# Cross-attention on one core: batch results transposed by VectorE and ScalarE instead of TensorE

## The chip, the cores and the metric

The kernel runs on one core of one Trainium2 chip. The metric is the device time of one execution in microseconds. The kernel before takes 938.81 us, the median of three runs (938.34 to 940.67).

The engines of the core are named as the profile names them: PE is TensorE's matrix products (PEld its weight loads), DVE is VectorE, ACT is ScalarE, POOL is GpSimd, SP is SyncE, which issues most transfers.

## What is computed

The reference works on 16 batches of 100 rows of 640 numbers (`x`) and 722 context rows of 384 numbers. The last 4 context rows of a batch are taken off as extra tokens (`ca`), and 718 remain (`enc`). There are 8 heads of 80 columns.

```python
query = hidden_states @ Wq
keyt = enc @ Wk
valt = enc @ Wv
hs = _mha(query, keyt, valt)
ca_q1 = jnp.einsum('btc,th->bch', ca, Wq_ca)
ca_q1 = ca_q1[:, indices, :]
ca_hs1 = _mha(ca_q1, residual, residual)
ca_q2 = ca_hs1 @ Wq
ca_k2 = ca @ Wk_ca
ca_v2 = ca @ Wv_ca
ca_hs2 = _mha(ca_q2, ca_k2, ca_v2)
out = hs + ca_hs2
out = out @ Wout + b_out
out = out + residual
```

Everything is float32. What this text is about is the step between the last two parts: `hs + ca_hs2` of a batch lies with its 100 rows on partitions, and the product with `Wout` needs it transposed, with the 640 columns on partitions, in 5 chunks of 128.

## The kernel before

**The loop.** After a first part that loads and combines the weights, one loop runs over the batches (line 1195). The order of the instructions inside it is written out by hand: each engine runs its own queue in the order of the program text. Iteration b works on the scores of batch b, forms the values of batch b and the keys of batch b + 1, and puts away the result of batch b - 1 (`last`). Its order on TensorE is:

1. the scores of batch b in three groups (`scores`, L623); ScalarE copies them to SBUF (L634, L640);
2. small products of the second attention (`softmax2`, `products`; L811, L749);
3. in iterations 2 to 15: the transposes of batch b - 1's result (`last.transpose`, L931). Five products with an identity, one for each chunk of 128 columns, write one PSUM bank, `hst_ps`; ScalarE copies it into `hsT` (L944), in one copy, or in two where a block of 128 output rows ends inside the batch. Iteration 1 does this later, near its end, for batch 0;
4. values and keys, 15 + 15 block products of 4 matrix products each (`Values`, L443, and `Keys`, L474);
5. the last chunk of the keys (L568); after every third iteration or so, the output product of two blocks of 128 rows (`project_pair`, L1010); in odd iterations the queries of the next two batches (L544);
6. probabilities times values (L1410). VectorE divides by the sums into `hs` (L1424) and adds `hs2`, the result of the second attention (L1431).

**Values and keys.** The products of `V_PLAN` are called V0 to V14 here, those of `K_PLAN` K0 to K14. Each names a PSUM bank or pair of banks (A to E), into which it adds, and a place in `vs` or `kT`. After each product the bank's present sum is read: by a ScalarE copy where the place is written for the first time (L416), by a VectorE addition otherwise (L414). The next product on the same bank has to wait for that read. The banks in order are

- V: A, B, D, A, B, E, A, B, C, A, C, B, A, B, A
- K: A, B, D, A, B, A, E, B, A, B, C, A, C, B, A

ScalarE reads V0, V1, V2, V8, V9, V14 and K0, K1, K2, K8, K9, K14; VectorE reads the rest. Banks A and B of V are a pair from the pool that also holds the first and the third group of scores.

**The maximum.** While these run, VectorE forms the maximum over all keys of each query (`Maximum`, `top`): a transpose in 32x32 blocks (L675), reductions (L677 to L687), then ScalarE spreads the result (`spread`, L697), and VectorE transposes it back into `over` (L705). `subtract` takes `over` from the scores (L1217), `exponential` follows on ScalarE (L1225). The calls `top.go(n)` in the loop set where these steps stand, and `both(n)` issues n products of V and then n of K:

```python
top.go(3)
both(3)
now.scores2()
top.go(1)
both(2)
top.go()
both(2)
both(1)
now.softmax3()
now.values2()
```

The first `top.go(3)` goes as far as the reductions, `top.go(1)` is `spread`, and `top.go()` is `over`. `softmax3` ends with `p2` (L862), which `values2` on GpSimd needs (L876, L883); it fills `hs2`, a buffer of which there is one.

**The rest of `last`.** `hsT` has three buffers of 128 rows each. When two blocks are complete (`PAIRS`), GpSimd forms sums of them (`sums`, L991) and TensorE multiplies them by `Wout` (`project_pair`).

Of the kernel before, what the change touches and what calls it, by code (L numbers as in the profile page):

```python
# [8 lines left out]
F32 = mybir.dt.float32  # L9
# [5 lines left out]
B, S, H = 16, 100, 640  # L15
# [3 lines left out]
P = 128  # L19
HC = H // P  # L20
# [12 lines left out]
OC = [(r, P) for r in range(0, B * S - P - 64, P)] + [(B * S - P - 64, 64), (B * S - P, P)]  # L33
# [7 lines left out]
HT = NH * T  # L41
# [12 lines left out]
for h in range(NH):  # L54
    lo = h * D
    while lo < (h + 1) * D:
        c = lo // P
        hi = min((h + 1) * D, (c + 1) * P)
        PIECES.append((h, c, lo - h * D, lo - c * P, hi - lo))
        lo = hi  # L60
# [75 lines left out]
def kernel(  # L136
# [18 lines left out]
    nc = tc.nc  # L155

    const = ctx.enter_context(tc.tile_pool(name="const", bufs=1))
    inp = ctx.enter_context(tc.tile_pool(name="inp", bufs=2))
    qpool = ctx.enter_context(tc.tile_pool(name="qpool", bufs=1))
    main = ctx.enter_context(tc.tile_pool(name="main", bufs=1))  # L160
# [22 lines left out]
    turn = [0]  # L183
# [10 lines left out]
    def scores_tile(name):  # L194
        return main.tile([P, 2, ROWS], F32, tag="st", name=name, bufs=NP)

    def hs_tile(name):
        return main.tile([P, H], F32, tag="hs", name=name)

    def hs2_tile(name):  # L200
        return main.tile([P, H], F32, tag="hs2", name=name)

    def hsT_tile(name):
        return main.tile([P, HC, P], F32, tag="hsT", name=name, bufs=3)

    def xn_tile(name):
        return main.tile([P, H], F32, tag="xn", name=name, bufs=2)
# [50 lines left out]
        tc.keep_in_program_order(dma)  # L258


    wv_sb = const.tile([P, NF, H // 2], F32, name="wv_sb")
    wk_sb = const.tile([P, NF, 2, P], F32, name="wk_sb")
    wk4 = const.tile([P, CC, P], F32, name="wk4")
# [79 lines left out]
    for c in range(HC):  # L343
        first = c * P - HEADS[c][0] * D
# [13 lines left out]

    room_v = xn_tile("wv_there")
    wv_there = {5: bias[:, : H // 2], 14: bias[:, H // 2 :], 7: room_v[:, : H // 2]}  # L360
    m_sb = [t[:, : B * HT] for t in (hs_tile("m_0"), xn_tile("m_1"), hs2_tile("m_2"))]
    m_sb += [
        hsT_tile(f"m_{c}").rearrange("p c s -> p (c s)")[:, : B * HT] for c in range(3, HC)
    ]
# [528 lines left out]
    hsTs = {}  # L893

    spare = []

    class Last:
# [20 lines left out]
        def parts(self, n):  # L918
# [2 lines left out]
                return [(0, slice(0, H))]  # L921
            return [(64 * k, slice(k * (H // 2), (k + 1) * (H // 2))) for k in range(2)]

        def transpose(self, chunks=[(0, HC)]):
            b, hs = self.b, self.hs
            if not self.t_ps:
                self.t_ps = psumk(f"hst_ps_{b}")
            t_v = self.t_ps[:, : HC * S].rearrange("p (c s) -> p c s", c=HC)
            for c0, c1 in chunks:
                for c in range(c0, c1):  # L930
                    nc.tensor.transpose(  # L931
                        t_v[:, c], hs[:S, c * P : (c + 1) * P], ident[:S, :S]
                    )
                for r, (lo, n) in enumerate(OC):
                    first, end = max(lo, b * S), min(lo + n, (b + 1) * S)
                    if first >= end:
                        continue
                    if r not in hsTs:
                        hsTs[r] = (
                            spare[0].rearrange("p (c s) -> p c s", c=HC)  # L940
                            if r == len(OC) - 1
                            else hsT_tile(f"hsT_{r}")
                        )
                    nc.scalar.copy(  # L944
                        hsTs[r][:, c0:c1, first - lo : end - lo],
                        t_v[:, c0:c1, first - b * S : end - b * S],
                    )

# [134 lines left out]
    for n in range(HC):  # L1083
        for c in range(CC):
            for lo in (0, 64):
# [5 lines left out]
                    stop=(c == CC - 1),  # L1091
                )
    k2T, at = [], 0
# [12 lines left out]
    for c in range(HC):  # L1106
        m_ps = psum(f"m_ps_{c}")
        for n, heads in enumerate(HEADS):
# [5 lines left out]
                stop=(n == HC - 1),  # L1114
# [46 lines left out]
    for c in range(CC):  # L1161
        for n in range(2):
# [5 lines left out]
                stop=(c == CC - 1),  # L1168
# [17 lines left out]
    last, enc_next, second_next = None, load_rest(1, load_enc(1)), Second(1, xT)  # L1186
# [8 lines left out]
    for b in range(B):  # L1195
        p = b // 2
        e_in, now = enc, second
        enc, second = enc_next, second_next
        mine = Last(b)
# [55 lines left out]
        if b == 0:  # L1255
            second.scores1()
            m_next = load_m(b + 2)
            kk.go(3)
            top.go(3)
            first_values(3, e_in, (act, act), get=bank)  # L1260
            top.go(1)
            kk.go(2)
            now.scores2()
            first_values(0, e_in, (act, act), (0,), bank)
            top.go()
            kk.go(3)
            first_values(0, e_in, (act, act), (1,), bank)
            now.softmax3()
            kk.go(2)
            subtract(0)  # L1270
            exponential(0)
            kk.go(2)
            subtract(1)
            kk.go(3)
            exponential(1)
            second_next, enc_next = loads()
            less = subtract(2)
            exponential(2)
            last_keys(b + 1, enc)
            enc_next = load_rest(b + 2, enc_next)  # L1280
            keys(m_next)
            now.values2(less)
            enc_sums(enc_next)
            second.softmax1(4)
        elif b + 1 < B:
            if b > 1:
                last.transpose()
            vv = Values(b, e_in)

            def both(n):  # L1290
                vv.go(n)
                kk.go(n)

            forms = [wout_sb[:, 2 * i : 2 * i + 2, k * (H // 2) : (k + 1) * (H // 2)]
                     for i in range(2) for k in range(2)]
            if b == 2:
                for o, left, right in (
                    (forms[1], forms[1], forms[0]),
                    (wout2[:, 0], forms[3], forms[1]),
                    (wout2[:, 1], forms[2], wout2[:, 0]),  # L1300
                ):
                    nc.gpsimd.tensor_tensor(o, left, right, ALU.subtract)
            elif last.b - 1 in PAIRS:
                nc.gpsimd.tensor_tensor(wout2[:, 0], wout2[:, 0], forms[0], ALU.add)
            second.scores1(seen)
            if b == 1:
                now.load()
            last.load()
            top.go(3)
            both(3)  # L1310
            now.scores2()
            top.go(1)
            both(2)
            top.go()
            both(2)
            both(1)
            now.softmax3()
            if b == 1:
                nc.gpsimd.tensor_tensor(last.hs[:S], last.hs[:S], last.hs2, ALU.add)
            now.values2()  # L1320
            if last.b in PAIRS:
                last.sums()
            vv.go(2)
            kk.go(1)
            subtract(0)
            exponential(0)
            vv.go(1)
            subtract(1)
            vv.go(1)
            kk.go(2)  # L1330
            exponential(1)
            vv.go(1)
            kk.go(2)
            both(1)
            both(1)
            if b == 1:
                for f in list(wv_there):
                    nc.scalar.copy(wv_sb[:, W_AT[f]], wv_there.pop(f))
            second.load()
            if b == 1:  # L1340
                nc.gpsimd.dma_start(out=bias, in_=bout[0].partition_broadcast(P))
            second_next, enc_next = loads()
            if b + 2 < B:
                m_next = load_m(b + 2)
            subtract(2)
            exponential(2)
            last_keys(b + 1, enc)
            if b + 2 < B:
                enc_next = load_rest(b + 2, enc_next)
            if b == 1:  # L1350
                last.transpose()
            if last.b in PAIRS:
                second.softmax1(3)
                last.project_pair()
                if last.b == max(PAIRS):
                    nc.sync.dma_start(
                        out=forms[1],
                        in_=wout[: 2 * P, H // 2 :].rearrange("(c p) n -> p c n", p=P),
                    )
            second.softmax1()  # L1360
        else:
            room = enc_tile("spare").rearrange("p f k -> p (f k)")
            spare.extend(room[:, i * H : (i + 1) * H] for i in range(2))
            last.transpose()
            vv = Values(b, e_in)
            last.load()
            mine.load()
            top.go(3)
            vv.go(3)
            last.project_few(len(OC) - 2)  # L1370
            now.scores2()
            top.go(1)
            vv.go(2)
            top.go()
            vv.go(3)
            now.softmax3()
            now.values2()
            vv.go(2)
            subtract(0)
            exponential(0)  # L1380
            vv.go(5)
            for i in (1, 2):
                subtract(i)
                exponential(i)
            last.project()
# [7 lines left out]
        if 0 < b < B - 1:  # L1393
            second.exponentials1()

        mine.hs = hs = hs_tile(f"hs_{b}")
        hs2 = now.hs2
        for g in range(2):
            a_ps = psum1(f"a_ps_{b}_{g}")
# [5 lines left out]
            for h, i in order:  # L1405
# [3 lines left out]
                for lo, hi in QC:  # L1409
# [5 lines left out]
                        stop=(i == len(KC) - 1),  # L1415
# [14 lines left out]
            if b:  # L1430
                nc.vector.tensor_tensor(hs[:S, cols], hs[:S, cols], hs2[:, cols], ALU.add)  # L1431
        mine.hs2 = hs2
        last = mine

    last.project(range(1))
# [53 lines left out]
```

## Time and profile before

| | |
|---|---|
| median of three runs | 938.81 us |
| profiled execution | 940.45 us |
| its span | 938.7 us |
| TensorE transposes L931, all 80 | 9.8 us busy, 251 ns each |
| copies of their result L944, 29 | 0.19 to 0.60 us each |
| block transposes of the maximum L675, L705 (128x800) | 1.01 us each |
| additions in `hs`, L1431 | 0.49 us each |
| VectorE waits for the first scores, L1241 | 49.1 us in 16 waits |
| GpSimd waits for `p2`, L876 | 41.2 us in 9 waits |

The span is the time from the first to the last instruction of the program. Busy times are sums over the engine's instructions; products of TensorE overlap, so that their busy time is more than the distance from one to the next. In a timeline, a row is a run of like instructions: start, time that they took together, engine, line, operation, output and inputs, shape, how many; in brackets stands the idle time of the engine just before, and what ended it.

### The profile page before, as it was taken

To read this page: it belongs to the slowest core of one execution; us is meant where nothing else is said; L and a number is where in the kernel's file an instruction comes from. 1 tells how busy PE (TensorE), PEld (TensorE's weight loads), DVE (VectorE), ACT (ScalarE), POOL (GpSimd) and SP (SyncE) were. 2 spreads that over 40 slices of the span, in tenths; PEclk is the share of its full clock that TensorE was granted. 3 is DMA by queue.
4 is the path that set the end of the run, shared out by engine and by line. 5 is a ranking of instruction groups with operands and counts; after the bars stand their busy time and mean duration, and the time that the engine had idled before them with its cause. 6 is when DMAs were issued, how large, how long until landed. Compare 5 with 4: busy or idle time off the path is not lost.

```text
span 938.7 us, 25800 instructions
## 1 busy us (share of the span) xinstructions
PE 929.9 (99%) x11195; PEld 792.8 (84%) x11195; DVE 687.9 (73%) x1098; ACT 372.6 (40%) x615; POOL 671.8 (72%) x614
## 2 busy tenths in 40 slices
PE   8999999999999999999999999999999999999998
PEld 6997979797797979888798788988879888798866
DVE  3859794989739796685957859589783897738884
ACT  1235443434334343442424434254441534415341
POOL 5757998688937878496874968658795587956723
PEclk9999999999999999999999999999999999999999
DMA  8822022040300303031030401205030050310201
GB/s 258 264 84 75 25 78 63 8 146 2 106 26 21 106 12 120 2 106 49 29 102 3 124 31 30 75 1 153 3 101 31 1 153 2 102 44 2 81 16 44
DMA packets 49672, 62.82 MB, mean 67 GB/s; under 512 B 14072, under 2 KB 38200, under 8 KB 49560
## 3 DMA queue, kind: packets, MB, share of 16 engines
q1 hardware_dynamic: 45512, 51.49, 18.2%
q0 software_dynamic: 3024, 8.53, 2.9%
q8 instruction: 88, 1.44, 0.6%
q10 hardware_dynamic: 1024, 1.15, 0.4%
q14 instruction: 24, 0.20, 0.1%
HBM read 55.59 MB, written 5.57 MB: 65 GB/s over the span
## 4 chain that ended last, share of the span: by engine, by line
PE 96%; DVE 2%; issue 1%; DMA 1%; ACT 0%; POOL 0%; ACTq 0%; DVEq 0%
PE s_ps L623 12%; PE a_ps L1410 12%; PE v_psA L443 10%; PE v_psB L443 8%; PE kT_ps L568 8%; PE k_psA L474 7%; PE q_ps L544 7%; PE k_psB L474 6%; PE o_ps L1010 5%; PE v_psC L443 3%; PE k_psC L474 3%; PE y_ps L749 2%; PE v_ps L384 2%; PE v_psD L443 2%; PE v_psE L443 2%; PE k_psE L474 1%
## 5 line engine op out<-in xcount | busy, mean ns | idle before, releaser
L784 POOL TENSOR_TENSOR e<-ca,g 100x800 f32<-100x800 f32 x64 | 99.5, 1565 | 137.2 <-DVE most L1229 123.6
L876 POOL TENSOR_TENSOR hs<-vb,p 100x640 f32<-100x640 f32 x64 | 120.5, 1892 | 50.4 <-DVE p L862 41.2
L509 POOL TENSOR_TENSOR enc<-enc 128x240 f32<-128x240 f32 x135 | 104.5, 783 | 20.0 <-DMA enc<-in_enct 12.9
L1410 PEld LDWEIGHTS a_ps<-vs,st 120*36 120x36 f32 (+3 forms) x3072 | 109.2, 125 | 4.9 <-issue 4.8
L1410 PE MATMUL a_ps<-vs,st 120*36 120x81 f32 (+3 forms) x3072 | 111.9, 233 | 0.0
L443 PE MATMUL v_psA<-wv_sb,enc 128*120 128x320 f32 x352 | 109.5, 434 | 0.0
L1217 DVE TENSOR_TENSOR st<-st,over 120x1600 f32<-120x1600 f32 x48 | 104.4, 2177 | 0.0
L883 POOL TENSOR_TENSOR hs<-hs,hs 100x640 f32<-100x640 f32 x48 | 99.1, 2064 | 3.8
L623 PE MATMUL s_ps<-qp,kT 32*120 32x100 f32 x3072 | 98.9, 263 | 0.6 <-issue 0.6
L623 PEld LDWEIGHTS s_ps<-qp,kT 32*120 32x120 f32 x3072 | 96.0, 179 | 2.4 <-issue 1.0
L791 POOL TENSOR_TENSOR e<-e,e 100x800 f32<-100x800 f32 x48 | 92.3, 1923 | 3.8
L443 PE MATMUL v_psB<-wv_sb,enc 128*120 128x320 f32 x296 | 91.9, 433 | 0.0
L640 ACT COPY st<-s_ps 120x800 f32<-120x800 f32 x64 | 49.7, 829 | 100.4 <-PE s_ps L623 100.4
L474 PE MATMUL k_psA<-enc,wk_sb 128*128 128x240 f32 x360 | 87.7, 366 | 0.0
L1229 DVE TENSOR_TENSOR most<-most,st 120x800 f32<-120x800 f32 x64 | 67.7, 1058 | 23.3 <-ACT st L634 22.2
L1225 ACT ACTIVATE st<-st 120x1600 f32<-120x1600 f32 x48 | 73.8, 1538 | 22.9 <-DVE st L1217 22.9
L474 PEld LDWEIGHTS k_psA<-enc,wk_sb 128*128 128x128 f32 x360 | 68.2, 190 | 16.8 <-DVE kT L414 0.3
L443 PEld LDWEIGHTS v_psA<-wv_sb,enc 128*120 128x120 f32 x352 | 63.2, 183 | 22.6 <-issue 0.5
L474 PE MATMUL k_psB<-enc,wk_sb 128*128 128x240 f32 x300 | 73.1, 366 | 0.3 <-DVE sm L859 0.3
L443 PEld LDWEIGHTS v_psB<-wv_sb,enc 128*120 128x120 f32 x296 | 54.1, 183 | 21.9 <-DVE vs L414 0.4
L544 PE MATMUL q_ps<-xT,wq_sb 128*128 128x200 f32 x400 | 69.1, 333 | 0.0
L544 PEld LDWEIGHTS q_ps<-xT,wq_sb 128*128 128x128 f32 x400 | 67.8, 190 | 1.0 <-issue 0.5
(162 smaller groups left out, 1734.6 us busy)
## 6 DMA issues: line engine op xcount, KB each, us to landing
vb<-va_d POOLq DMA_DIRECT2D x32, 250.0 KB, 3.6
vb<-va_d SPq DMA_DIRECT2D x32, 250.0 KB
enc<-in_enct SPq DMA_DIRECT2D x30, 240.0 KB
enc<-in_enct SPq DMA_DIRECT2D x15, 360.0 KB
xT<-in_xt SPq DMA_DIRECT2D x8, 500.0 KB
rest<-in_enct SPq DMA_DIRECT2D x31, 120.0 KB
xn<-in_x SPq DMA_DIRECT2D x11, 320.0 KB
out<-xn SPq DMA_DIRECT2D x11, 320.0 KB
```

The costliest lines, as they stand in the source:

```text
L443: nc.tensor.matmul(at[0][j][:KN, : H // 2], a_form(self.enc, f)[:, j * KN : (j + 1) * KN], wv_there.get(f, wv_sb[:, W_AT[f]]), start=first ...
L474: nc.tensor.matmul(at[:, i * KT : (i + 1) * KT], wk_sb[:, W_AT[f], i], a_form(self.enc, f), start=(first and i == 0), stop=last, skip_grou ...
L509: nc.gpsimd.tensor_tensor(out, left, right, op)
L544: nc.tensor.matmul(q_ps[:, : 2 * S].rearrange("p (j s) -> p j s", j=2), wq_sb[:, c, n * P : (n + 1) * P], xT[:, :, c, :], start=(c == 0), ...
L568: nc.tensor.matmul(bank[:, i * KT : (i + 1) * KT], weights[c], a_raw(enc, u, c), start=(i == 0 and c == 0), stop=(c == CC - 1), skip_group ...
L623: nc.tensor.matmul(s_ps[r][:n, 256 * a + lo : 256 * a + hi], kT[rows, c, u, j * KN : (j + 1) * KN], rhs, start=(a == 0 and c == 0), stop=( ...
L784: first = nc.gpsimd.tensor_tensor(to, self.ca[:, t, :].unsqueeze(1).to_broadcast([S, NH, S]), g[:, :, t].unsqueeze(2).to_broadcast([S, NH, ...
L791: nc.gpsimd.tensor_tensor(e, e, to, ALU.add)
L876: first = nc.gpsimd.tensor_tensor(to, self.vb[t][:S].rearrange("p (h d) -> p h d", h=NH), p2[:, :, t].unsqueeze(2).to_broadcast([S, NH, D] ...
L883: nc.gpsimd.tensor_tensor(sums, sums, to, ALU.add)
L1217: return nc.vector.tensor_tensor(st[i], st[i], top.over[:KN].unsqueeze(1).to_broadcast([KN, 2, ROWS]), ALU.subtract,)
L1410: nc.tensor.matmul(a_v[lo:hi, h % 4], st[i // 2][: KEYS[i], i % 2, h * S + lo : h * S + hi], block(i, h // 4)[: KEYS[i], h % 4], start=(i ...
```

## The change

The results of batches 1 to 13 no longer go through TensorE.

- `hs` becomes one fixed tile, `hs_sb`, of 128 rows. Its rows from 96 on are cleared once in the columns that no early use of the tile fills (`m_0` of the first part lies in it).
- After the last addition to `hs` of batches 1 to 13, VectorE transposes the whole tile in 32x32 blocks into `turned`, which takes a buffer of the tag `hs2`.
- In iterations 2 to 14, ScalarE copies the blocks to their places in `hsT`: for each of the 4 groups of 32 rows and each of the 4 groups of 32 partitions, one copy of 32 partitions and 5 runs of up to 32 elements. A group of rows that lies across the end of a block of 128 output rows is copied in two parts.
- The call of `last.transpose()` at the beginning of iterations 2 to 14 goes. Batches 0, 14 and 15 are transposed as before.
- `place` stands behind `spread`. The two calls `both(2)` become one `both(4)`, and `top.go()`, which is `over`, comes behind it. This holds for iterations 1 to 14.

```diff
+    hs_sb = const.tile([P, H], F32, name="hs_sb")
+    nc.gpsimd.memset(hs_sb[96:, B * HT :], 0.0)
...
+        def turn(self):
+
+            self.turned = hs2_tile(f"turned_hs_{self.b}")
+            nc.vector.transpose(self.turned, self.hs)
+
+        def place(self):
+
+            turned = self.turned.rearrange("p (c m k) -> p c m k", m=4, k=32)
+            for i in range(4):
+                at = self.b * S + 32 * i
+                stop = min(at + 32, (self.b + 1) * S)
+                for r, (lo, n) in enumerate(OC):
+                    first, end = max(lo, at), min(lo + n, stop)
+                    if first >= end:
+                        continue
+                    for m in range(4):
+                        nc.scalar.copy(
+                            self.hsT(r)[32 * m : 32 * m + 32, :, first - lo : end - lo],
+                            turned[32 * i : 32 * i + 32, :, m, first - at : end - at],
+                        )
...
         elif b + 1 < B:
-            if b > 1:
-                last.transpose()
             vv = Values(b, e_in)
...
             both(3)
             now.scores2()
             top.go(1)
-            both(2)
+            if b > 1:
+                last.place()
+            both(4)
             top.go()
-            both(2)
             both(1)
             now.softmax3()
...
-        mine.hs = hs = hs_tile(f"hs_{b}")
+        mine.hs = hs = hs_sb
...
         mine.hs2 = hs2
+        if 0 < b < B - 2:
+            mine.turn()
         last = mine
```

`self.hsT(r)` gives the buffer of block r, as the lines that it replaces in `transpose` did.

## What the change does to the time: a prediction

> **What bounds the kernel now.** I read the engine totals first, then the chain that ended last, then the timelines of TensorE, VectorE and ScalarE in one iteration of the batch loop, iteration 4 (the one that works on batch 4 and puts away batch 3). The first view is parts 1 and 4 of the page.
>
> ```profile
> PE 929.9 (99%) x11195; PEld 792.8 (84%) x11195; DVE 687.9 (73%) x1098; ACT 372.6 (40%) x615; POOL 671.8 (72%) x614
> ...
> PE 96%; DVE 2%; issue 1%; DMA 1%; ACT 0%; POOL 0%; ACTq 0%; DVEq 0%
> ```
>
> TensorE (PE) is busy for 99% of the span, and 96% of the chain is TensorE. So a product taken off it shortens the run, unless another engine then makes it wait. The question is who stands next in line, and that is read from iteration 4. First TensorE's timeline (start, time, engine, line, operation):
>
> ```profile
> 281.33 0.59 PE L931 MATMUL hst_ps<-ident,hs 100*128 100x100 f32 x5
> 281.76 1.26 PE L443 MATMUL v_psA<-wv_sb,enc 128*120 128x320 f32 x4
> ...
> 287.44 1.24 PE L443 MATMUL v_psA<-wv_sb,enc 128*120 128x320 f32 x4
> 288.51 1.24 PE L443 MATMUL v_psB<-wv_sb,enc 128*120 128x320 f32 x4
> 289.59 0.97 PE L474 MATMUL k_psA<-enc,wk_sb 128*128 128x240 f32 x4
> 290.40 0.97 PE L474 MATMUL k_psB<-enc,wk_sb 128*128 128x240 f32 x4
> ...
> 292.29 1.24 PE L443 MATMUL v_psA<-wv_sb,enc 128*120 128x320 f32 x4
> 293.36 0.97 PE L474 MATMUL k_psA<-enc,wk_sb 128*128 128x240 f32 x4
> ```
>
> The five transposes show 0.59 us, but the next product starts 0.43 us after them: 281.33 to 281.76. That is what they hold TensorE. The rows from 287.44 are V3, V4, K3, K4, V6 and K5 of the two plans. A V product costs 1.08 us from start to start, a K product 0.81.
>
> VectorE's timeline of the same stretch:
>
> ```profile
> 288.99 0.81 DVE L414 TENSOR_TENSOR vs<-v_psA,vs 120x640 f32<-120x640 f32 x1
> 289.90 0.82 DVE L414 TENSOR_TENSOR vs<-v_psB,vs 120x640 f32<-120x640 f32 x1
> 290.67 0.66 DVE L414 TENSOR_TENSOR kT<-k_psA,kT 128x480 f32<-128x480 f32 x1
> 291.43 0.66 DVE L414 TENSOR_TENSOR kT<-k_psB,kT 128x480 f32<-128x480 f32 x1
> 292.01 1.00 DVE L705 STREAM_TRANSPOSE over<-spread 128x800 f32<-128x800 f32 x1
> 292.93 0.85 DVE L414 TENSOR_TENSOR vs<-v_psE,vs 120x320 f32<-120x320 f32 x2
> 293.89 0.83 DVE L414 TENSOR_TENSOR vs<-v_psA,vs 120x640 f32<-120x640 f32 x1
> ```
>
> V3 ended at 288.68 (287.44 + 1.24); VectorE reads it at 288.99, 0.31 us late, since it comes from the reduction of the maximum. It runs through without a pause. VectorE is thus a third of a microsecond behind TensorE, with no wait to be seen yet, because each bank has time until its next product.
>
> ScalarE's timeline, and two of its copies from SBUF to SBUF by source line (count: shortest/median/longest ns):
>
> ```profile
> 289.23 1.71 ACT L697 COPY spread<-mx 64x800 f32<-64x800 f32 x2
> 297.61 0.96 ACT L416 COPY vs<-v_psC 120x320 f32<-120x320 f32 x2 [6.67 <-PE v_psC L443]
> ```
>
> ```profile
> L697 ACT COPY spread<-mx x42: 841/856/862, 77.2 to 905.5; 64x800 f32<-64x800 f32 x42
> L1338 ACT COPY wv_sb<-bias x2: 460/460/461, 138.2 to 138.5; 128x320 f32<-128x320 f32 x2
> ```
>
> After `spread` ScalarE is idle for 6.67 us. The copies of `place` go into that gap.
>
> **What is removed.** Thirteen times five transposes (iterations 2 to 14). The trace gives 0.43 us from the first to the next product in each of these (0.49 in iteration 15, which keeps its own): 13 x 0.43 = 5.6 us at most. Not all of it can be had at once: V0 writes a bank pair whose last reader, ScalarE's copy of the scores at L640 (279.77 + 1.55 = 281.32), ends just where the transposes began. With 0.06 us from the end of a read to the next product (K12 in iteration 3 starts 0.05 after the read that it waited for), V0 can start 0.38 earlier, not 0.43. ScalarE loses its one or two copies at L944 (0.6 us); it is not on the path.
>
> The Trainium skill ("TensorE: Matmul & The Clock Gate", Part 4: PE-mode transpose) gives about 275 ns for a transpose inside a kernel. By that figure 65 of them would be an estimated 17.9 us; this trace has them 0.086 us apart, and the sum goes by the trace.
>
> **What is added.** (a) VectorE's `turn`, 128x640: the nearest row is the same operation on 128x800 (L675) at 1.01 us, so 0.81 us by size, 13 times. It stands behind the last addition to `hs`, where VectorE next waits 2.4 to 2.9 us for the first scores (L1241 in iterations 3 to 5). Cost nothing; without that cover 0.8 us on the maximum, hence on V3's read. (b) `place`: 16 copies of 32 partitions, 20 where a block of 128 rows ends inside the batch (it does in nine of thirteen; 244 in all). The two rows give (856 - 460)/480 = 0.83 ns an element and 0.196 us fixed. Four times 500 elements make 1.66 us; 20 fixed parts 3.9 us; in sum 5.6 us. The copies at L1338 start 0.36 apart though they last 0.46, so neighbours may overlap by 0.10: 3.7 us. The two at L697 do not overlap, so I take 5.6. It begins at 290.94 and ends at 296.5. Queued behind it on ScalarE are the two copies of V8's banks, which V10 waits for, then V9, K8 and the first exponential. V8 will come some 0.3 earlier, at 297.3: hidden. V10 starts at 299.5 or later and the two copies take 0.96, so `place` may last 7.5 us before TensorE waits: 0.38 us a copy. (c) GpSimd's `values2` writes the buffer that `turned` sits in, so it waits for `place`; but it waits for `p2` anyway, which ends after 298. Nothing. (d) A memset of 32x128 on GpSimd at the start: 32x800 takes 0.76 there (L368), so under 0.2 us; GpSimd then idles 9.8 us before L721. Nothing. No DMA is added or moved.
>
> **What is moved.** Two things, both in `both(4)`. VectorE's `over` goes behind K6's read, past V5, V6, K5 and K6; it is needed by the first `subtract`, which stays behind V7 and K7, so the order alone costs that nothing. And V5 and V6 go ahead of K3 and K4, on TensorE and on VectorE. That is the part that costs: K3's bank is wanted again by K5 after K4 alone, where before V5 and V6 lay between. In offsets from V0 in the before, K5 stands at 11.61 in both orders. VectorE's reads now run V3, V4, V5, V6, K3 and take 0.91 + 0.74 + 0.96 + 0.74 + 0.65 = 4.00 us from V3's start (spacings of rows as above; 0.74 from V4 to another target is iteration 3's, where nothing holds VectorE up). They start at 6.92 plus the lag. So K5 can start at 6.92 + lag + 4.00 + 0.06, and the gain that is left is 0.63 - lag, no more than 0.38. VectorE's start is set by the scores and does not come forward when the transposes go.
>
> The lags of V3's read, from the timelines: 0.30 to 0.32 in iterations 2, 4, 6 to 10, 12 and 14; 0.24 in 11, 0.26 in 13; 0.84 in 3, 0.73 in 5, where VectorE's maxima last 1.4 us instead of 1.0; 1.43 in 1. So: nine iterations at 0.32 make 2.9 us; iterations 11 and 13 give 0.38 and 0.37; iteration 3 loses 0.21 but no longer pays the 0.16 that its K12 waited; iteration 5 loses 0.10. Iteration 1 has no transposes to lose but takes the new order: K5 is 0.80 later, of which 0.35 was already paid at K6; 0.4 lost. Sum: 2.9 + 0.75 - 0.05 - 0.10 - 0.4 = 3.1 us.
>
> The profiled execution took 940.45 us (span 938.7 and 1.75 around it); it would take 937.3. The median of the three runs is 938.81, 0.17% lower; less 3.1 it is **935.7**.
>
> **A rule against the change.** The Trainium skill ("VectorE: DVE Perf Modes", rules for kernel authors) sends a 128x128 transpose to TensorE where its result may lie in PSUM, as it may here. Followed to the letter it would say to leave things alone: by the rows above, 0.43 us of TensorE and 0.6 of ScalarE become 0.8 of VectorE and up to 5.6 of ScalarE. Which counts depends on who is idle, and that the page does not weigh.
>
> **The rivals.**
> - *All of it comes through.* K5's wait does not show, because VectorE passes from bank to bank faster in the new order, and V0 starts at once. 13 x 0.43 = 5.6 us: 933.2. For it: at the typical lag the wait is under 0.1 us. Against it: ScalarE's copy ends only just before V0, and iterations 1, 3 and 5 are late.
> - *VectorE eats it.* If lags of 0.6, as between the typical and iterations 3 and 5, become the rule (GpSimd's sums fall elsewhere against VectorE's maxima), 0.63 - lag is nothing and iteration 1 still loses 0.4: 939.2. Against it: nine of thirteen lags agree within 0.02.
> - *ScalarE becomes the bound (slower).* Place: V10, waiting for V8's two copies behind `place`. Point: 0.38 us a copy; to be slower by 0.3% needs about 0.41. At 0.45, nine iterations wait 20 x 0.45 - 7.5 = 1.5 us, 13.5 in all, less 3.1: 949.2. For it: 0.196 us fixed, no overlap at L697, and no row of copies between unlike partitions. Against: the smallest copies of the trace (L944) take 0.19.
>
> **Chances.** Under 0.3%, 2.8 us, a measurement of this kernel can't be told from no change. My forecast has 0.50 with a range of its own of 934.4 to 936.9 (0.1 us more or less of lag in each of 13 iterations); 936.0 is the limit of faster, so 0.32 of it counts as faster and 0.18 as the same. All of it: 0.24. VectorE eats it: 0.09. ScalarE: 0.17. Faster 0.56, same 0.27, slower 0.17. The range goes from 932.9 (all of it, with 0.3 us of spread) to 939.8 (nothing left, with 1 us).
>
> **What would show it.** V0 follows the last y product with no row at L931 in iterations 2 to 14; a gap of up to 0.1 us before K5 at the typical lag, larger in iterations 1, 3 and 5; no idle time before V10; `place` ends before V8's copies; `turn` lies inside VectorE's wait for the first scores. A mean over 0.38 us from copy to copy, or a lag of V3's read that grows by more than the 0.38, proves me wrong.

## The result, and the profile after

| kernel | median | fastest to slowest | ratio |
|---|---|---|---|
| before | 939.61 us (7 runs) | 938.12 to 941.32 | |
| after | 942.87 us (7 runs) | 942.26 to 943.54 | 1.0035 [1.0023, 1.0046] |

The change makes the kernel slower by 0.35%, 3.3 us. I had forecast 935.7 us. The profiled execution of the kernel after took 943.54 us, with a span of 941.8 (before: 938.7). Some line numbers moved: V products are L442, K products L473, VectorE's reads of them L413, ScalarE's L415, `over` L704, `p2` L861, `subtract` L1240, `values2` L875 and L882, `turn` L935, `place` L948.

Parts 1 and 4 of the page of after:

```profile
PE 930.6 (99%) x11130; PEld 785.7 (83%) x11130; DVE 698.5 (74%) x1111; ACT 434.6 (46%) x836; POOL 674.1 (72%) x615
...
PE 85%; DVE 12%; issue 2%; ACT 1%; DMA 0%; POOL 0%; ACTq 0%; DVEq 0%
```

TensorE lost its 65 transposes, and ScalarE gained 62 us of copies. What tells most is the chain: VectorE's share went from 2% to 12%. TensorE now waits for it somewhere.

Where, the waits show (engine, tile and line; what it waited for; us in total, times, longest). In the before, no wait of a K product for VectorE sums to more than 0.3 us:

```profile
PE k_psA L473 <- DVE kT L413: 2.2, 6, 0.4
...
PE k_psC L473 <- DVE kT L413: 0.7, 2, 0.3
```

The list shows only part of it: it counts the time from the end of one row to the start of the next, and in an even pace these rows overlap by 0.16 us (a K product lasts 0.97 and the next starts after 0.81). Below, K4 ends at 459.88 and K5 starts at 459.99, 0.11 by that count, but 0.27 behind the pace. The timeline of TensorE in iteration 7 of after, in two stretches, K3 to K6 and V12 to K12 (the view ends inside K12, hence x3):

```profile
458.10 0.97 PE L473 MATMUL k_psA<-enc,wk_sb 128*128 128x240 f32 x4
458.91 0.97 PE L473 MATMUL k_psB<-enc,wk_sb 128*128 128x240 f32 x4
459.99 1.05 PE L473 MATMUL k_psA<-enc,wk_sb 128*128 128x240 f32 x4
460.87 0.97 PE L473 MATMUL k_psE<-enc,wk_sb 128*128 128x240 f32 x4
...
470.31 1.24 PE L442 MATMUL v_psA<-wv_sb,enc 128*120 128x320 f32 x4
471.38 0.97 PE L473 MATMUL k_psA<-enc,wk_sb 128*128 128x240 f32 x4
472.42 0.88 PE L473 MATMUL k_psC<-enc,wk_sb 128*128 128x240 f32 x3
```

A K product costs 0.81 us from start to start. K4 to K5 takes 1.08 and K5 to K6 0.88: 0.27 of waiting and 0.07 to regain the pace. K11 to K12 takes 1.04: 0.23 of waiting. VectorE in the same iteration, with everything between K3's read and K10's that matters here:

```profile
458.42 0.82 DVE L413 TENSOR_TENSOR vs<-v_psA,vs 120x640 f32<-120x640 f32 x1
459.18 0.66 DVE L413 TENSOR_TENSOR kT<-k_psA,kT 128x480 f32<-128x480 f32 x1
...
462.46 1.00 DVE L704 STREAM_TRANSPOSE over<-spread 128x800 f32<-128x800 f32 x1
...
465.10 0.19 DVE L861 TENSOR_TENSOR p<-e,sm 100x32 f32<-100x32 f32 x1
465.20 1.82 DVE L1240 TENSOR_TENSOR st<-st,over 120x1600 f32<-120x1600 f32 x1
468.22 2.85 DVE L1240 TENSOR_TENSOR st<-st,over 120x1600 f32<-120x1600 f32 x1
...
471.72 0.64 DVE L413 TENSOR_TENSOR kT<-k_psC,kT 128x480 f32<-128x480 f32 x1
```

K3's read ends at 459.84 and K5 starts at 459.99; K10's read ends at 472.36 and K12 starts at 472.42. Both waits are for the reads named. The first read is late because K3's product, which now stands behind V5 and V6, is done only at 459.07 (458.10 + 0.97); the read starts at 459.18, while V6's read (458.42) is still running. The second is late because it stands behind the second `subtract`, which ends at 471.07 (468.22 + 2.85).

The balance over all iterations, from the starts of the first scores product, of V0 and of K14 in both traces (after less before, us). Iteration 7 stands for 2, 4, 9, 10 and 12, all within 0.01:

| iteration | 1 | 3 | 5 | 6, 8 | 7 | 11 | 13 | 14 |
|---|---|---|---|---|---|---|---|---|
| scores to V0 | -0.03 | -0.43 | -0.14 | -0.43 | -0.43 | -2.24 | -0.80 | -0.43 |
| V0 to K14 | +1.11 | +0.67 | +1.25 | +0.34 | +0.64 | +0.68 | +0.76 | +0.95 |

The transposes bring 13 x 0.43 = 5.6 us, but the stretch from V0 to K14 loses 10.0 in the fourteen iterations. That makes +4.4. The rest is single pauses that differ between the two profiled executions: beyond their 0.43, iterations 11 and 13 show 2.2 us that the profile of before alone spent, in pauses of TensorE for which it names no cause ("issue"); after has one of 0.91 at the end of iteration 4 and loses 0.29 in iteration 5, and its loop starts 0.3 earlier. Together: +3.1, the difference of the spans.

### The profile page after: what moved, and what is told of

Read it like the earlier page. It is cut to its first block, busy times and chain, and to the rows that moved or that the text cites. A ratio compares the mean times of both kernels' runs of the same rounds, so it can differ in the third digit from the quotient of the medians.

```text
span 941.8 us, 25879 instructions
## 1 busy us (share of the span) xinstructions
PE 930.6 (99%) x11130; PEld 785.7 (83%) x11130; DVE 698.5 (74%) x1111; ACT 434.6 (46%) x836; POOL 674.1 (72%) x615
## 4 chain that ended last, share of the span: by engine, by line
PE 85%; DVE 12%; issue 2%; ACT 1%; DMA 0%; POOL 0%; ACTq 0%; DVEq 0%
PE a_ps L1432 12%; PE s_ps L622 11%; PE kT_ps L567 8%; PE v_psA L442 8%; PE q_ps L543 7%; PE v_psB L442 7%; PE k_psA L473 6%; PE o_ps L1033 5%; PE k_psB L473 5%; PE v_psC L442 3%; DVE vs L413 3%; DVE st L1240 2%; PE k_psC L473 2%; DVE most L1252 2%; PE v_ps L383 2%
## 5 line engine op out<-in xcount | busy, mean ns | idle before, releaser
L875 POOL TENSOR_TENSOR hs<-vb,p 100x640 f32<-100x640 f32 x64 | 119.8, 1881 | 53.1 <-DVE p L861 24.1
L442 PE MATMUL v_psA<-wv_sb,enc 128*120 128x320 f32 x352 | 110.0, 435 | 0.3
L1240 DVE TENSOR_TENSOR st<-st,over 120x1600 f32<-120x1600 f32 x48 | 107.1, 2234 | 0.0
L882 POOL TENSOR_TENSOR hs<-hs,hs 100x640 f32<-100x640 f32 x48 | 100.6, 2096 | 3.8
L442 PE MATMUL v_psB<-wv_sb,enc 128*120 128x320 f32 x296 | 91.8, 433 | 0.0
L473 PE MATMUL k_psA<-enc,wk_sb 128*128 128x240 f32 x360 | 88.7, 369 | 3.0 <-DVE kT L413 2.2
L473 PEld LDWEIGHTS k_psA<-enc,wk_sb 128*128 128x128 f32 x360 | 67.1, 190 | 22.3 <-issue 4.3
L442 PEld LDWEIGHTS v_psA<-wv_sb,enc 128*120 128x120 f32 x352 | 62.8, 183 | 24.4 <-DVE vs L413 2.9
L473 PE MATMUL k_psB<-enc,wk_sb 128*128 128x240 f32 x300 | 73.1, 366 | 0.3 <-DVE sm L858 0.3
L442 PEld LDWEIGHTS v_psB<-wv_sb,enc 128*120 128x120 f32 x296 | 54.1, 183 | 21.9 <-DVE vs L413 0.4
L1444 DVE RECIPROCAL rs<-a_ps 100x4 f32<-100x4 f32 x32 | 5.8, 180 | 86.0 <-PE a_ps L1432 86.0
```

Of the source, the lines that this page charges most:

```text
L442: nc.tensor.matmul(at[0][j][:KN, : H // 2], a_form(self.enc, f)[:, j * KN : (j + 1) * KN], wv_there.get(f, wv_sb[:, W_AT[f]]), start=first ...
L473: nc.tensor.matmul(at[:, i * KT : (i + 1) * KT], wk_sb[:, W_AT[f], i], a_form(self.enc, f), start=(first and i == 0), stop=last, skip_grou ...
L875: first = nc.gpsimd.tensor_tensor(to, self.vb[t][:S].rearrange("p (h d) -> p h d", h=NH), p2[:, :, t].unsqueeze(2).to_broadcast([S, NH, D] ...
L882: nc.gpsimd.tensor_tensor(sums, sums, to, ALU.add)
L1240: return nc.vector.tensor_tensor(st[i], st[i], top.over[:KN].unsqueeze(1).to_broadcast([KN, 2, ROWS]), ALU.subtract,)
```

## The experiments

Medians are set against the kernel before as measured beside them: 939.63 us (17 runs) for kernels 1 to 4 and 939.21 us (10 runs) for 5 to 8. "Kernel 1" is that of experiment 1, and so on. "Typical" is an iteration like 7.

**1. The change with the old order.** `place` and `turn` stay; the order of the products and of `over` is that of the before.

```diff
-            both(4)
-            top.go()
+            both(2)
+            top.go()
+            both(2)
```

> The changed kernel with the order of before: both(2), over, both(2), both(1); turn and place stay. Theory A (the new order costs): K5 and K12 wait no longer, so V0 to K14 lasts as before (27.5 us in most iterations) while the transposes stay away; 0.43 us in some ten of thirteen iterations, 934 to 935.5 us, ratio 0.994 to 0.996 of before. Rival B (the new work of VectorE and ScalarE costs, whatever the order): 942 to 943 us, as the changed kernel.

936.4 us, ratio 0.9964 [0.9951, 0.9978]: 3.2 us faster than before, 0.9 above the range that I expected. From V0 to K14 a typical iteration takes the time of the before to within 0.01, so it gains the whole 0.43; K5 stands 11.61 us after V0 and K12 23.74, as in the before. Not the full 5.6 us come, because iterations 3 (+0.64), 5 (+0.51), 11 (+0.55), 13 (+0.37), 14 (+0.35), 6 and 8 (+0.17) lose some from V0 to K14. In iteration 3, K6 waits 0.41 for V5's read and K12 0.29: V0 has come forward by 0.43 and VectorE, held by the maxima, has not. These losses come to 2.8 us. So it is the order that makes the change slow, not its new work.

**2. The order alone.** The kernel before, with `both(4)` and then `top.go()`, and TensorE's transposes kept.

```diff
-            both(2)
-            top.go()
-            both(2)
+            both(4)
+            top.go()
```

> The kernel before with the new order alone: both(4), over, both(1); transposes on TensorE, no turn, no place. Theory A: slower than before without any new work. Iteration 1 loses 1.1 us as in the changed kernel; in the others the lag of 0.31 leaves K5 free, but over comes later, p2 is 0.4 us later, GpSimd's values2 with it, and K12 waits 0.2 to 0.3 us; in all 3 to 5 us, 942.5 to 944.5 us. Rival B: the order costs iteration 1 alone, 939.5 to 940.7 us.

948.15 us, ratio 1.0094 [1.0079, 1.0109]: 8.5 us slower than before. Less the 5.6 us of the transposes that is 2.9, near the 3.3 of the whole change. It costs about twice what I expected, and I had K5 free. The reason is in TensorE's and VectorE's timelines of iteration 7 (K3, K4 and K5; the reads of V6 and K3):

```profile
459.75 0.97 PE L474 MATMUL k_psA<-enc,wk_sb 128*128 128x240 f32 x4
460.56 0.97 PE L474 MATMUL k_psB<-enc,wk_sb 128*128 128x240 f32 x4
461.64 1.05 PE L474 MATMUL k_psA<-enc,wk_sb 128*128 128x240 f32 x4
```

```profile
459.95 0.82 DVE L414 TENSOR_TENSOR vs<-v_psA,vs 120x640 f32<-120x640 f32 x1 [0.42 <-PE v_psA L443]
460.83 0.66 DVE L414 TENSOR_TENSOR kT<-k_psA,kT 128x480 f32<-128x480 f32 x1
```

V0 starts at 449.77 here, so V3's read (457.00) is 7.23 after it, as in the before: the lag is the old 0.31. Yet K5 waits 0.27. VectorE idles 0.42 us until V6's product is done, reads it by 460.77, and starts K3's read at 460.83. So VectorE is not late at all. It is K3's product that comes late: it ends at 460.72, and the read follows 0.11 behind it. In the eight iterations of after in which K5 starts 11.87 or 11.88 after V0 it is the same, though the lag is 0.73 there: V6's read starts between 10.29 and 10.30 after V0, in kernel 2 at 10.19, but K3's read always at 11.07, 0.11 after K3's product. (Where an idle VectorE waits for a product, as for V6's here, the read starts 0.04 after its end. The other 0.07 may be owed to V6's read in front; the traces don't tell.) So at lags from 0.22 to 0.74 the wait doesn't depend on the lag. The order of the products sets it: from the end of K3 to K5's due start there are 0.65 us, and a read takes 0.66.

**3. Only `over` late.** The change with V5, V6, K3 and K4 in the old order, and `over` behind K6.

```diff
-            both(4)
+            both(2)
+            both(2)
             top.go()
```

> The changed kernel with both(2), both(2), over, both(1): V and K products alternate as before, over alone stays late. Theory A in two parts: K5 does not wait (that part came from V5 and V6 ahead of K3), K12 still waits some 0.3 us (that part comes from the late over, through p2 and values2); 936.5 to 939 us. If the order of the products were all of the cost: 934 to 935.5. If over's place were all of it, or if it is rival B: 942 to 943.

937.69 us, ratio 0.9977 [0.9968, 0.9986], as expected: 1.3 us above kernel 1, where `over` is early, and 5.2 below after, where V5 and V6 go first. K5 stands at 11.61 again with no wait. But a typical iteration still loses 0.30 of its 0.43, and all of that at K12 (0.22 of waiting and 0.08 until the pace is back). VectorE and GpSimd in iteration 7:

```profile
459.25 1.00 DVE L704 STREAM_TRANSPOSE over<-spread 128x800 f32<-128x800 f32 x1
460.17 0.78 DVE L413 TENSOR_TENSOR vs<-v_psB,vs 120x640 f32<-120x640 f32 x1
460.88 0.64 DVE L413 TENSOR_TENSOR kT<-k_psB,kT 128x480 f32<-128x480 f32 x1
...
461.88 0.19 DVE L861 TENSOR_TENSOR p<-e,sm 100x32 f32<-100x32 f32 x1
461.99 1.82 DVE L1240 TENSOR_TENSOR st<-st,over 120x1600 f32<-120x1600 f32 x1
...
465.01 2.85 DVE L1240 TENSOR_TENSOR st<-st,over 120x1600 f32<-120x1600 f32 x1
```

```profile
462.21 3.96 POOL L875 TENSOR_TENSOR hs<-vb,p 100x640 f32<-100x640 f32 x2 [2.10 <-ACT vs L415]
466.25 3.02 POOL L882 TENSOR_TENSOR hs<-hs,hs 100x640 f32<-100x640 f32 x1
```

The same steps in iteration 7 of the before, where V0 starts at 445.15 (`p2`, the two `subtract`, `values2`):

```profile
461.49 0.19 DVE L862 TENSOR_TENSOR p<-e,sm 100x32 f32<-100x32 f32 x1
461.59 1.82 DVE L1217 TENSOR_TENSOR st<-st,over 120x1600 f32<-120x1600 f32 x1
...
464.91 2.55 DVE L1217 TENSOR_TENSOR st<-st,over 120x1600 f32<-120x1600 f32 x1
```

```profile
461.75 4.02 POOL L876 TENSOR_TENSOR hs<-vb,p 100x640 f32<-100x640 f32 x2 [2.19 <-DVE p L862]
```

In kernel 3 `over` now stands in front of V7's and K7's reads, and behind these stand the steps of `softmax3` that end in `p2` and the first `subtract`. With V0 at 445.24, `p2` starts 16.64 after V0 instead of 16.34. From there a fixed train runs. `values2` on GpSimd and the first `subtract` start behind `p2`, 0.22 apart (the profile names ScalarE as what `values2` waited for, since it also waits for `place`; but in kernels 1 and 3 and in after alike it starts 0.13 after `p2` ends); the two products of `values2` end 2.36 us after that `subtract` (466.17 after 463.81); the second `subtract`, begun while they run, ends 1.69 after them (467.86); K10's read follows. In the before the same distances are 2.36 and 1.69, in after 2.37 and 1.68. So whatever `p2` loses, K10's read loses: 0.30 here, 0.65 in after (0.30 from `over`, 0.35 from K5). In the before K12 came 0.13 after the read it needed, so there was little slack to eat. Over the whole program a late `over` costs less than 0.30 an iteration on average, because V5's read now goes ahead of it: K6 no longer waits in iterations 1, 3 and 5, and these are shorter than in kernel 1.

**4. `values2` behind the second `subtract`.** The change as it is, but GpSimd starts later.

```diff
             now.softmax3()
-            now.values2()
...
+            now.values2(subtract(1))
+            if last.b in PAIRS:
+                last.sums()
```

> The changed kernel, with GpSimd's values2 of iterations 1 to 14 held back until the second subtract has ended. Theory A: K12 waits because subtract and values2 run at the same time and hold each other up; then the second subtract falls from 2.85 to about 1.8 us and K12's wait goes (0.3 us in ten iterations), K5's stays: 939.5 to 940.5 us, unless the later hs2 makes the end of an iteration wait. If the subtract is long for another reason: 2.85 us and K12's wait stay, 942.5 to 944 us.

946.01 us, ratio 1.0065 [1.0051, 1.0078]. VectorE and GpSimd in iteration 7:

```profile
467.34 1.82 DVE L1240 TENSOR_TENSOR st<-st,over 120x1600 f32<-120x1600 f32 x1
470.36 1.81 DVE L1240 TENSOR_TENSOR st<-st,over 120x1600 f32<-120x1600 f32 x1
```

```profile
472.30 2.50 POOL L875 TENSOR_TENSOR hs<-vb,p 100x640 f32<-100x640 f32 x2 [7.21 <-issue]
474.89 1.54 POOL L882 TENSOR_TENSOR hs<-hs,hs 100x640 f32<-100x640 f32 x1
```

Apart from each other, the `subtract` takes 1.81 us, the two products 2.50 instead of 3.97, the sum 1.54 instead of 3.01. K12's wait is gone: a typical V0 to K14 loses 0.32 instead of 0.64, and that is K5's part (its wait stays, 0.26). The mechanism holds, but the total went the other way: the sums for `project_pair` now stand behind `values2`, and the output product of iterations 3, 6, 8, 11 and 13 takes 0.77 to 2.07 us longer, with waits for these sums (L1014) and for what GpSimd makes after them (L1054). (The profiled execution also has a pause of 1.45 us put down to "issue" ahead of V0 of iteration 3; it took 947.38, 1.4 above the median.)

**5. `over` between V5 and V6.** The order of kernel 1, but with V5, on TensorE and on VectorE, ahead of `over`:

```diff
-            both(4)
-            top.go()
+            both(2)
+            vv.go(1)
+            top.go()
+            vv.go(1)
+            kk.go(2)
```

> The run with the old order (936.4 us), with over moved behind V5's read alone: both(2), V5, over, V6, K5, K6, both(1). Theory A: the typical iteration stays as it is (no wait there); in iterations 1, 3, 5, 11 and 13, where VectorE is over 1 us late, K6 no longer waits for V5's read (0.3 to 0.5 us each) and p2 keeps its time; 934 to 935.5 us. If over's place mattered only through p2: 936.4 as before.

935.4 us, ratio 0.9961 [0.9949, 0.9974]: as expected, and the lowest median of all. Its chain by engine:

```profile
PE 95%; DVE 2%; POOL 1%; issue 1%; DMA 0%; ACT 0%; DVEq 0%; POOLq 0%
```

TensorE has nearly its share of the before again. V5's read ahead of `over` frees pair E for K6, so the late iterations gain too (iteration 1 -0.42 from V0 to K14 against the before, 3 -0.26, 5 -0.02). Some of it comes back in 3, 11 and 13, where the output product starts on time but takes 0.7 to 0.9 us longer. In iteration 3 it falls 0.42 behind its pace at a product that needs GpSimd's sums (L1014) and 0.32 at one that needs `wout2`, which GpSimd makes after them (L1054); that is all of its 0.74. Its interval overlaps that of kernel 1, so that it is better than kernel 1 is not shown by the times.

**6. The same, with `values2` late and the sums ahead of it.** The edit of kernel 4 on top of kernel 5, with `last.sums()` left where it was.

> The same, and GpSimd's values2 held back behind the second subtract, with the sums of the output pair ahead of it, so that project_pair needn't wait for them. Theory A: the second subtract takes 1.8 us instead of 2.5, K12's wait goes in iterations 3, 5, 11 and 13 (0.3 each), and the wait of 0.8 to 2 us behind K14 that values2's delay alone brought in iterations 3, 6, 8, 11 and 13 goes as well; 932.5 to 934.5 us. If hs2 comes too late now for the end of an iteration: 936 to 940.

935.81 us, ratio 0.9962 [0.9949, 0.9976]. A miss: no better than kernel 5. My premise was wrong: in kernel 5 K12 no longer waits in iterations 3, 5, 11 and 13 either, so that a typical iteration gains no more than 0.03 beyond its 0.43. And while the output product no longer waits for the sums, GpSimd's later step for it (L1054) now comes after the delayed `values2`: in iteration 6 it ends 11.01 us after K14's start, the product that needs it starts at 11.06, and the output product takes 0.2 to 0.6 us longer in the iterations that have one.

**7. `place` cut short.** Kernel 1 with one or two ScalarE copies of all 128 partitions in place of the 16 or 20; the output rows of batches 1 to 13 are then not those of the reference, since the blocks are not put in their places.

```diff
-                    for m in range(4):
-                        nc.scalar.copy(
-                            self.hsT(r)[32 * m : 32 * m + 32, :, first - lo : end - lo],
-                            turned[32 * i : 32 * i + 32, :, m, first - at : end - at],
-                        )
+            nc.scalar.copy(
+                self.hsT(r)[:, :, first - lo : end - lo],
+                turned[:, :, first - self.b * S : end - self.b * S],
+            )
```

> The run with the old order, with place cut to one or two copies over 128 partitions (what ScalarE had to copy before), so the blocks are not put into their transposed places and the output rows of batches 1 to 13 are not the reference's. Theory A: ScalarE's 5.7 us are hidden, so 936.0 to 936.8 us as with the 20 copies. Rival B: the 20 copies cost; at 0.1 to 0.2 us an iteration 934 to 935.

936.29 us, ratio 0.9969 [0.9958, 0.9981], as expected, the time of kernel 1. ScalarE's busy time is 375.1 us instead of 434.5, and nothing comes of it: `place` is hidden.

**8. `place` half as long again.** Kernel 1 with two of the four copies of each group done twice.

```diff
-                    for m in range(4):
+                    for m in (0, 1, 2, 3, 0, 1):
```

> The run with the old order, with half as many copies again in place (two of each four are made twice; the result is the same). 30 copies last 8.5 us, from 9.6 to 18.1 after V0; V8's two copies end at 19.1, and V10, due at 18.08, waits 1.1 us in the nine iterations with 30 copies, not at all in the four with 24 (they end at 16.5): 10 us more, 945 to 948.5 us. If ScalarE has more room than that: under 940. If the copies hold up more than V10: over 952.

942.37 us, ratio 1.0035 [1.0022, 1.0049]: 6.0 us above kernel 1, and below the 945 to 948.5 that I expected. ScalarE and TensorE, iteration 7 (the last number in brackets is idle time and what ended it):

```profile
456.10 8.71 ACT L948 COPY hsT<-turned_hs 32x160 f32<-32x160 f32 x30
464.83 0.76 ACT L415 COPY vs<-v_psC 120x320 f32<-120x320 f32 x2
```

```profile
463.74 0.97 PE L473 MATMUL k_psA<-enc,wk_sb 128*128 128x240 f32 x4
465.31 1.34 PE L442 MATMUL v_psC<-wv_sb,enc 128*120 128x320 f32 x4 [0.60 <-ACT vs L415]
```

V10 waits for V8's copies behind `place`, 0.76 us beyond the pace (465.31 less 463.74 is 1.57, and a K product takes 0.81), and V0 to K14 is 0.53 to 1.06 longer than in kernel 1 in the nine iterations with 30 copies (0.83 in four of them), and no longer in the four with 24. The third rival's mechanism and its place are real; it needs only more copies than the change has. Its limit lies nearer 8.0 us of `place` (8.71 less 0.76) than the 7.5 of the prediction, and I had expected 1.1 us a time. V10's first matrix product needs only the first of the two copies, so it starts at 465.31, before they end at 465.59.

## Why the prediction was wrong

Of the forecast's five steps three hold in the main and two failed, and the two that failed are both in `both(4)`. A smaller error lies in the lags that it started from.

- *What is removed: 0.43 us an iteration, capped at 0.38.* The 0.43 is right, the cap wrong. In iteration 7 of after the scores' copy ends at 448.10 and V0 starts at 448.11, so all 0.43 comes (0.05 more in thirteen iterations, 0.65 us more than in my sum).
- *`turn`: 0.81 us, hidden.* It takes 0.845 in all 13, and VectorE idles 2.00 us after it in iteration 7. Right.
- *`place`: 5.6 us for 20 copies, hidden while a copy takes under 0.38.* It takes 5.67, 0.28 us a copy, as ScalarE's timeline of after shows in the row below. V10 does not wait, and cutting `place` (kernel 7) changes nothing. That neighbouring copies don't overlap was the right one of the two assumptions.

```profile
457.76 5.67 ACT L948 COPY hsT<-turned_hs 32x160 f32<-32x160 f32 x20
```

- *`over` moved: "the order alone costs that nothing".* **Failed.** I asked who needs `over` and found the first `subtract`, behind V7 and K7. I did not ask what stands behind `over` in VectorE's queue: V7's and K7's reads, and behind them `p2`. Kernel 3 prices this step alone at 0.30 us in a typical iteration, by way of GpSimd's `values2` and K10's read. The sentence that `values2` "waits for `p2` anyway" named the link and treated it as cover.
- *V5 and V6 ahead of K3 and K4: gain left 0.63 less the lag.* **Failed.** I made K5's wait out of VectorE's backlog alone: 4.00 us of reads from V3's start to the end of K3's. I left out when K3's product itself is done. In the new order that is 10.96 after V0; K3's read starts 0.11 later, takes 0.66, and K5 starts 0.15 behind it, at 11.87 or 11.88, where the pace wants 11.61: 0.27, and 0.08 more until K6 is on its pace. I had 0.11 in all, with 0.06 for the 0.15. In iteration 7 of after both limits fall together, since the reads I had counted take 4.06 us there and also bring K3's read to 11.07; kernel 2 tells them apart. So the wait is not a matter of the lag: it is there in kernel 2 at a lag of 0.31 as in after at 0.74, and in kernel 3, without V5 and V6 moved, there is none. Only where VectorE is later still (lags of 1.12 to 1.41 in iterations 1, 3, 5, 11 and 13 of after) does its backlog add to it, and K5 starts at 12.21 to 12.51. (In iteration 14 of after, K5 stands at 12.18 with a lag of 0.74: VectorE idles 0.46 us ahead of V6's read there, and the profile doesn't show why.)
- *The lags of iterations 11 and 13.* My sum also took 0.38 and 0.37 of gain from these two, for their small lags of 0.24 and 0.26. They were small in that one profile, in which TensorE had just paused there (the 2.2 us above). In after, without these pauses, the lags are 1.12 and 1.19, and the two iterations take 0.25 and 0.33 longer than in the before, pauses aside.

Together 0.35 and 0.30 an iteration make +0.64 against the -0.43, as the table shows; I had +0.11 against them. By the medians the regrouping of the products weighs more than the late `over`: kernel 3 is 1.3 us above kernel 1, after is 5.2 above kernel 3. Kernel 1, with both undone, is 3.2 us faster than before, where I forecast 3.1. That agreement is luck: the loss at K5 that I had counted in isn't there (K5 stands at 11.61), and 2.8 us go in other places, at K6 and K12 of the late iterations above all, which I had not counted.

Of the rivals, *all of it comes through* is nearest in kernels 1 and 5, 0.3% to 0.4% faster. *VectorE eats it* named the engine but not the cause: in nine iterations the lag grew by 0.41 to 0.44, which is what V0 comes earlier (in 3, 5, 11 and 13 by 0.53 to 0.93), and kernel 1 with such lags is faster than before; the new order did the rest; in *ScalarE becomes the bound* the threshold was not reached. None had the change lose on its own new order.

## What to carry to other kernels

When an instruction is moved back in an in-order queue, price everything that it now stands in front of, not only the one that needs it: here a transposition of 1.00 us pushed a multiplication of 0.19 us (`p2`) by 0.30, and that moved GpSimd and, two links further on, TensorE. When products are regrouped over few PSUM banks, write down for each product when the last read of its bank can start at the earliest, from the end of the product that is read as well as from the reader's backlog: K5 follows K3 after K4 alone, and the read doesn't fit between them even when VectorE is free. And run the new work in the old order before judging it: here the two parts of one edit are worth -0.36% and +0.94%.

## What the runs showed of the hardware

- A two-input VectorE operation on 120x1600 takes 1.81 to 1.82 us alone, and 2.55 to 2.85 in iteration 7 of the kernels where GpSimd had begun its 100x640 products first. The rows agree with taking turns rather than sharing. In after, GpSimd's two products (465.42, 3.97 us) start under the first `subtract`, end at 469.39, and the second `subtract`, begun at 468.22, ends 1.68 after them, about its time alone; GpSimd's sum (469.46, 3.01 us) ends 1.40 after that `subtract`, near its 1.54 alone. The Trainium skill ("SBUF — State Buffer", section "Who interferes with whom") says that a VectorE instruction with two inputs in SBUF and a GpSimd instruction that reads SBUF contend, and calls the lock on the port pair that they share exclusive. These rows bear it out.
- From the end of a read to the next product on its bank pair: 0.15 us at K5, 0.06 at K12, in the same iteration. After a wait, the next product still comes 0.07 to 0.10 late. Why the two differ is open.
- ScalarE's copies from SBUF to SBUF between unlike partitions: 0.320 to 0.326 us for 32x160, 0.202 to 0.207 for 32x20, and each starts 0.01 after the one before has ended, on average 0.28 apart in iteration 7.
- Single pauses of TensorE, put down to "issue", fall in different iterations in different profiles: 0.65 us in iteration 4 of after, 1.45 in iteration 3 of kernel 4, 1.48 in iteration 11 of kernel 6. They blur single profiles by up to 2 us; no run here explains them.
